# Block 0's low-rank adapters computed one batch at a time, in a fused adapter and feed-forward kernel

## The chip, the cores and the metric

The kernel runs on one core of one Trainium2 chip. The metric is the device time of one execution in microseconds (us), as the median of several runs. A profile is one execution recorded by the hardware; its span runs from the first to the last instruction of the program, and the execution's own time is a little longer than its span.

## What is computed

There are 8 batches of 256 tokens with 1024 features each. Every batch has an adapter number; two low-rank products (rank 16) with that adapter's matrices make the input of a gated feed-forward layer with 2752 hidden features, whose three inputs are rounded to 8-bit floating point. The result is added to `x`.

```python
def reference(x, adapter_ids, A, B, gate_w, up_w, down_w, scales...):
    Bx  = einsum('bni,bri->bnr', x, B[adapter_ids])      # 1024 -> 16
    c   = einsum('bnr,bor->bno', Bx, A[adapter_ids])     # 16 -> 1024
    q   = lambda v, s: clip(v / s, -448, 448).astype(float8_e4m3fn) * s
    gate_out = q(c, gate_in_scale) @ (gate_w * gate_w_scale).T
    up_out   = q(c, up_in_scale)   @ (up_w * up_w_scale).T
    hidden   = silu(gate_out) * up_out
    return x + q(hidden, down_in_scale) @ (down_w * down_w_scale).T
```

## The kernel before

All data is held transposed, features on the 128 partitions and tokens along the row. The 2048 tokens form four blocks `t` of 512 (`TB`), so a block holds two batches of 256 (`SEQ`). The 1024 features are eight groups `k` of 128 (`NH`); the 2752 hidden features are 22 chunks `c` (`NI`).

**Adapters of a block.** `times_b` (L483) multiplies x by the 16 rows of B. It puts four small products side by side on TensorE, each in its own quarter of 32 output rows; `quads` says which adapter, which tokens and which quarter. For block 0, `two_times_b` (L499) lets the quarters be (half of the batch) x (batch), 128 tokens each. The sums in PSUM (`bx`) are copied to `bm` in SBUF, once straight and once with the upper and lower quarters exchanged, since a quarter of `bm` must stand beside the quarter of `a_two` that it is multiplied with. `two_times_a` (L530) then makes the tiles `c`, eight of 512 columns for a block, and `round_to` (L523) rounds each to 8 bits in `xg[0]`, four on ScalarE (L528) and four on VectorE (L526).

**Loads.** `load_x` (L378) brings block 0's x in three pieces of 4, 3 and 1 groups `k` (`PIECES`, L39): 1 MB, 768 KB and 256 KB. `load_b` (L365) and `load_a_two` (L370) bring an adapter's B (68 KB) and A (two pieces of 32 KB, 16 rows each); their addresses hang on the adapter's number, which `adapter_of` (L362) reads into a register of the queue that will issue the transfer. `load_gate_up` (L385) brings a chunk of gate and up weights (`w_gu`, 1 MB; the first in two halves). All transfers are issued by SyncE (SP), in the order in which they are written, but for the numbers `ids` and the first B, which ScalarE issues:

```python
        load_x(0, 0)
        load_b(b_two[0], 0, adapter_of(0, nc.scalar), nc.scalar)
        second = adapter_of(1, nc.sync)
        load_b(b_two[0], 1, second, nc.sync)
        load_x(0, 4)
        load_a_two(0, 1, second)
        load_a_two(0, 0, adapter_of(0, nc.sync))
        load_x(0, 7)
        for c in range(NFIRST):
            load_gate_up(c, parts=1 if c else 2)
```

Every transfer signals one of eight completion semaphores, handed out in turn; a transfer that uses one again waits, on its issuing engine, until the transfer that had it before has landed. What stands behind it on that engine waits too.

**Order on TensorE.** Every matmul goes through `multiply` (L469), so all of them have line L470 in the profile, and TensorE keeps the written order (L633 to L653): 16 products of zeros 512 wide (`pass_time`, L472, tile `warm`), block 0's `two_times_b` with four more products of zeros after its fourth group, seven more, `two_times_a(0)`, then `gate_up(0, 0)`, which is chunk 0 for block 0, in four turns of two groups `k`; then chunks 1 to 4 for block 0, into the last of which block 1's `two_times_b` is put, block 1 likewise with the adapters of blocks 2 and 3, and then all other chunks for all blocks. Each `gate_up` is 16 matmuls of 512 columns.

**The down product.** For each group `k` of outputs, 21 matmuls and a rest per block go into `yd`; `finish` (L691) scales it, adds x on VectorE (L695) and issues the store of the tile. For the last group, x is loaded again by two transfers (L744 to L753) into the room of `xg`.

All tiles in PSUM come from one pool of eight buffers used in rotation.

Of the kernel before, what the change touches and what calls it, by code (L numbers as in the profile page):

```python
# [9 lines left out]
F32 = mybir.dt.float32  # L10
# [5 lines left out]
ALU = mybir.AluOpType  # L16
AX = mybir.AxisListType

P = 128
T = 2048  # L20
SEQ = 256
NB = 8
H = 1024
I = 2752
R = 16
NH = H // P
NI = (I + P - 1) // P
TAIL = I - (NI - 1) * P
TB = 512
# [6 lines left out]

KS = NH // 2

PIECES = ((4, 3, 1), (4, 3, 1), (NH,), (NH,))  # L39
FP8_MAX = 448.0  # L40

SAME_MAX = 240.0
# [14 lines left out]
    return ap.bitcast(U16)[..., 0::2]  # L57


def x_of(x4, t, k):  # L60

    first = 0
    for n in PIECES[t]:
        if k < first + n:
            break
        first += n
    at = (t * NH + first) * P * TB
    piece = x4[at : at + n * P * TB].rearrange("(p k n) -> p k n", p=P, k=n)
    return piece, first


def x_row(x4, t, k):
    piece, first = x_of(x4, t, k)
    return piece[:, k - first, :]


def gate_up_of(w_gu, c):
# [15 lines left out]
def general(  # L93
# [71 lines left out]
    def adapt(t, lora, b_sb, a_sb):  # L165
        bx = psum.tile([P, TB], F32, tag="ps", name="g_bx")
        for k in range(NH):
            xk = lora.tile([P, TB], F32, tag="xk", name="g_xk", bufs=2)
            nc.sync.dma_start(out=xk, in_=x_row(x4, t, k))
            nc.tensor.matmul(  # L170
                bx, lhsT=b_sb[:, k, :], rhs=xk, start=(k == 0), stop=(k == NH - 1)
            )
        bm = lora.tile([P, TB], F32, tag="bm", name="g_bm")
        for j in range(TB // SEQ):
            b = t * (TB // SEQ) + j
            nc.vector.tensor_scalar(
                bm[:, bass.ts(j, SEQ)],
                bx[:, bass.ts(j, SEQ)],
                mask[:, b : b + 1],
                None,  # L180
                ALU.mult,
            )
        for k in range(NH):
            c = psum.tile([P, TB], F32, tag="ps", name="g_c")
            nc.tensor.matmul(
                c, lhsT=a_sb[:, bass.ts(k, P)], rhs=bm, start=True, stop=True
            )
            for to, s in ((xg, GATE_IN), (xu, UP_IN)):
                v = work.tile([P, TB], F32, tag="v", name="g_v")
                nc.scalar.activation(v, c, AF.Copy, scale=inv[:, s : s + 1])  # L190
                quantize(to[:, k, :], v, P)
# [38 lines left out]
    def down(t, hid):  # L230
        for k in range(NH):
# [25 lines left out]
                    stop=(i == len(tail) - 1),  # L257
                )
            xr = work.tile([P, TB], F32, tag="g", name="g_xr")
            nc.sync.dma_start(out=xr, in_=x_row(x4, t, k))  # L260
            o = work.tile([P, TB], F32, tag="v", name="g_o")
            nc.vector.scalar_tensor_tensor(
                o, in0=y, scalar=down_s, in1=xr, op0=ALU.mult, op1=ALU.add
# [20 lines left out]
def adaln_ffn(  # L284
# [52 lines left out]
    with ExitStack() as fast:  # L337
# [2 lines left out]
        work = fast.enter_context(tc.tile_pool(name="work", bufs=3))  # L340


        xs = [acts.tile([P, NH, TB], F32, name=f"x{t}") for t in range(NTB)]
        xg += [acts.tile([P, NH, TB], FP8, name=f"xg{t}") for t in range(2, NTB)]


# [2 lines left out]

        b_two = [lora.tile([P, 2 * BROW + R], F32, name=f"b{t}") for t in range(2)]
        a_two = [lora.tile([P, H // 2], F32, name=f"a{t}") for t in range(2)]

        b_four = lora.tile([P, 4 * BROW + R], F32, name="b_four")
        a_four = lora.tile([P, H], F32, name="a_four")
        nc.gpsimd.memset(a_two[0], 0.0)
        nc.vector.memset(a_two[1], 0.0)
        for b, n in ((b_two[0], 2), (b_two[1], 2), (b_four, 4)):
            nc.vector.memset(b[:, n * BROW :], 0.0)  # L360

# [5 lines left out]
                out=b[:, i * BROW : (i + 1) * BROW], in_=b8[bass.ds(adapter * P, P), :]  # L367
            )

        def load_a_two(t, j, adapter):  # L370
            for g in range(2):
                row = 32 * (2 * g + j) + R * j
                nc.sync.dma_start(
                    out=a_two[t][row : row + R],
                    in_=a8[bass.ds(adapter * 2 * R + g * R, R), :],
                )

        def load_x(t, k):  # L378
            piece, first = x_of(x4, t, k)
            ks = slice(first, first + piece.shape[1])  # L380
            nc.sync.dma_start(out=xs[t][:, ks, :], in_=piece)

        w_of = {}

        def load_gate_up(c, parts=1):  # L385
# [5 lines left out]
                nc.sync.dma_start(out=w[:, bass.ts(i, n)], in_=src[:, bass.ts(i, n)])  # L391
            w_of[c] = w

        load_x(0, 0)
        load_b(b_two[0], 0, adapter_of(0, nc.scalar), nc.scalar)
        second = adapter_of(1, nc.sync)
        load_b(b_two[0], 1, second, nc.sync)


        load_x(0, 4)  # L400
        load_a_two(0, 1, second)
        load_a_two(0, 0, adapter_of(0, nc.sync))
        load_x(0, 7)
        for c in range(NFIRST):
            load_gate_up(c, parts=1 if c else 2)
        adapters = [adapter_of(2 + q, nc.sync) for q in range(6)]
        for j in range(2):
            load_b(b_two[1], j, adapters[j], nc.sync)
        for k in (0, 4, 7):
            load_x(1, k)  # L410
        for j in range(2):
            load_a_two(1, j, adapters.pop(0))

        for t in (2, 3):
            load_x(t, 0)
# [64 lines left out]
                    stop=(i == n - 1),  # L480
                )

        def times_b(bx, b, n, quads, between=None):  # L483


            for k in range(NH):
                for q, (i, row, t, cols) in enumerate(quads):
                    at = i * BROW + k * R - row
                    multiply(
                        bx[q][32 * q : 32 * (q + 1)],  # L490
                        lhsT=b[:, at : at + 32],
                        rhs=xs[t][:, k, cols],
                        start=(k == 0),
                        stop=(k == NH - 1),
                    )
                if between:
                    between(k)

        def two_times_b(t, between=None):  # L499


            n = SEQ // 2
            quads = [
                (j, R * j, t, slice(at, at + n))
                for half in range(2)
                for j in range(2)
                for at in (j * SEQ + half * n,)
            ]
            bx = [psum.tile([P, n], F32, tag="ps", name=f"bx{half}") for half in range(2)]
            times_b([bx[q // 2] for q in range(4)], b_two[t], n, quads, between)  # L510
            bm = lora.tile([P, 2, n], F32, tag="bm2", name="bm2", bufs=2)
            for other in range(2):
                for half, copy in enumerate((nc.vector.tensor_copy, nc.scalar.copy)):
                    to = half ^ other
                    tc.keep_in_program_order(
                        copy(  # L516
                            bm[64 * to : 64 * (to + 1), other],
                            bx[half][64 * half : 64 * (half + 1)],
                        )
                    )  # L520
            return bm

        def round_to(to, c, engine):  # L523
# [3 lines left out]
            else:  # L527
                nc.scalar.activation(to, c, AF.Copy, scale=scale, saturate=False)  # L528

        def two_times_a(t, bm):  # L530


            n = SEQ // 2
            for part in range(2):
                cs = [psum.tile([P, 2, SEQ], F32, tag="ps", name=f"c{q}") for q in range(4)]
                for other, i in product(range(2), range(2)):
                    for q in range(4):
                        rows = slice(32 * q, 32 * (q + 1))
                        multiply(
                            cs[q][:, i, bass.ts(q // 2 ^ other, n)],  # L540
                            lhsT=a_two[t][rows, bass.ts(2 * part + i, P)],
                            rhs=bm[rows, other],
                            start=True,
                            stop=True,
                        )
# [3 lines left out]
                    round_to(to, cs[q], nc.vector if q % 2 else nc.scalar)  # L549

        def four_times_b():
            quads = [(q, 0, 2 + q // 2, bass.ts(q % 2, SEQ)) for q in range(4)]
            bx = psum.tile([P, SEQ], F32, tag="ps", name="bx")
            times_b([bx] * 4, b_four, SEQ, quads)
            bm = lora.tile([P, SEQ], F32, tag="bm", name="bm", bufs=2)
            nc.vector.tensor_copy(bm, bx)
            return bm
# [73 lines left out]


        warm = psum.tile([P, TB], F32, tag="ps", name="warm")  # L633
        pass_time(warm, 16, TB)
        bm = two_times_b(0, lambda k: pass_time(warm, 4) if k == 3 else None)
        pass_time(warm, 7)
        two_times_a(0, bm)
        gate_up(0, 0, turns=(2, 2, 2, 2))
        for c in range(1, NFIRST - 1):
            gate_up(c, 0)  # L640
# [49 lines left out]

        def finish(k, t, cols, y, x):  # L691
            o = outs.tile([P, TB], F32, tag="o", name="o")[:, cols]
            at = slice(t * TB + cols.start, t * TB + cols.stop)
            tc.keep_in_program_order(
                nc.vector.scalar_tensor_tensor(  # L695
                    o, in0=y, scalar=down_s, in1=x, op0=ALU.mult, op1=ALU.add
                )
            )
            tc.keep_in_program_order(nc.sync.dma_start(out=outT[bass.ts(k, P), at], in_=o))
# [30 lines left out]
        for k in range(NH - 1):  # L730
# [9 lines left out]
            if last:  # L740
                ws_last = load_down(k + 1)
                x_last = []

                blocks = x4.rearrange("(t n) -> t n", t=NTB)  # L744
                srcs = (
                    blocks[:2, bass.ts(k + 1, P * TB)].rearrange("t (p n) -> p t n", p=P),
                    blocks[2:].rearrange("t (p k n) -> p t k n", p=P, n=TB)[:, :, k + 1, :],
                )
                for i in range(2):
                    x = xg[i].rearrange("p k n -> p (k n)").bitcast(F32)  # L750
                    x = x.rearrange("p (t n) -> p t n", n=TB)
                    x_last += [x[:, j, :] for j in range(2)]
                    nc.sync.dma_start(out=x, in_=srcs[i])  # L753
            first = k % 2 == 0
            if first:
                tiles = down_tiles(NTB)
# [128 lines left out]
```

## Time and profile before

| | |
|---|---|
| median of 3 runs | 476.82 us (476.09, 476.82, 476.93) |
| the profiled execution: its time, its span | 477.12 us, 475.3 us |
| TensorE busy with matmuls | 469.8 us (99% of the span), 2514 of them |
| ScalarE, VectorE busy | 192.5 us (40%), 105.6 us (22%) |
| first matmul of chunk 0 for block 0 starts | 12.58 us after the span's start |
| data moved | 53.44 MB, 112 GB/s over the span, about 400 GB/s from 3 us to 33 us |

Times within the profile are counted from the span's start. Busy shares are averages over the whole span; the change touches only the first 17 us, so it must be read in that stretch, from the order in time and from what each engine waits for.

### The profile page before, as it was taken

The page shows a single profiled execution, that of the slowest core. Times are in us where ns is not written, and L with a number is a line of the kernel's source. Part 1 is how long each engine was busy: PE and PEld are TensorE (multiplying, and loading weights), DVE is VectorE, ACT ScalarE, POOL GpSimd, SP SyncE. Part 2 cuts the span into 40 slices and gives each one's busy share as a digit, 9 for nine tenths or more (in the row PEclk, how much of TensorE's full clock was granted, in tenths as well). Part 3 has the DMA queues.
Part 4 walks back from the last instruction along what each step waited for, and adds up shares of the span by engine and source line. Part 5 has one row for each costly group of instructions (what it writes and reads, how often), then busy time and mean ns, then how long its engine had stood idle before and what let it go on. Part 6 is the DMA issues. An engine that isn't in the chain of part 4 may idle for free.

```text
span 475.3 us, 6009 instructions
## 1 busy us (share of the span) xinstructions
PE 469.8 (99%) x2514; PEld 217.0 (46%) x2514; DVE 105.6 (22%) x163; ACT 192.5 (40%) x249; POOL 1.0 (0%) x7
## 2 busy tenths in 40 slices
PE   8999999999999999999999999999999999999997
PEld 4454544444444444444444444444444444444444
DVE  1333432121212222121212212132120121031031
ACT  1322447995556654533454554359212022021000
POOL 0000000000000000000000000000000000000000
PEclk9999999999999999999999999999999999999999
DMA  8995013422222112222211111123335255063031
GB/s 291 406 405 186 1 48 133 176 88 90 88 88 89 24 66 89 90 88 88 90 30 60 44 62 56 61 83 123 103 146 161 64 185 161 22 213 114 3 116 66
DMA packets 13780, 53.44 MB, mean 112 GB/s; under 512 B 1650, under 2 KB 2930, under 8 KB 10674
## 3 DMA queue, kind: packets, MB, share of 16 engines
q1 hardware_dynamic: 13600, 52.92, 32.1%
q8 instruction: 21, 0.34, 0.3%
q14 instruction: 13, 0.11, 0.1%
q10 hardware_dynamic: 146, 0.07, 0.0%
HBM read 44.60 MB, written 8.39 MB: 111 GB/s over the span
## 4 chain that ended last, share of the span: by engine, by line
PE 96%; DMA 3%; SPq 0%; issue 0%; DVE 0%
PE y L470 62%; PE yd L470 31%; DMA w_gu<-w_gu 2%; PE c L470 1%; PE bx L470 1%; DMA x<-x 1%; DMA ids_i<-ids 0%; SPq L363 0%; SPq L366 0%; DVE o L695 0%; PE count L470 0%
## 5 line engine op out<-in xcount | busy, mean ns | idle before, releaser
L470 PE MATMUL y<-xg,w_gu 128*128 128x512 fp8e4 x1376 | 298.4, 379 | 0.9 <-DMA w_gu<-w_gu 0.9
L470 PEld LDWEIGHTS <-w_gu 128*128 128x128 bf16 x1376 | 134.0, 98 | 163.8 <-DMA w_gu<-w_gu 1.8
L470 PE MATMUL yd<-hid,w_d 128*128 128x512 fp8e4 (+2 forms) x693 | 146.0, 373 | 0.0
L609 ACT ACTIVATE g<-y,gate_s 128x512 f32<-128x512 f32 (+1 forms) x88 | 59.8, 681 | 137.2 <-PE y L470 137.2
L610 DVE SCALAR_TENSOR_TENSOR hid<-y,up_by_down,g 128x512 fp8e4<-128x512 f32 x84 | 63.1, 751 | 220.3 <-PE y L470 162.2
L470 PEld LDWEIGHTS <-w_d 128*128 128x128 bf16 x693 | 66.6, 98 | 79.0 <-issue 1.7
L456 ACT ACTIVATE junk<-w_d 128x1408 bf16<-128x1408 uint16 (+1 forms) x16 | 21.2, 1324 | 88.4 <-DMA w_d<-w_d 88.3
L695 DVE SCALAR_TENSOR_TENSOR o<-yd,down_s,x 128x512 f32<-128x512 f32 x28 | 20.0, 748 | 107.4 <-PE yd L470 92.8
L456 ACT ACTIVATE junk<-w_gu 128x2048 bf16<-128x2048 uint16 (+1 forms) x22 | 41.0, 1863 | 0.0
L463 ACT ACTIVATE junk<-hid 128x2048 bf16<-128x2048 fp8e4 x21 | 40.0, 1905 | 0.4
L463 ACT ACTIVATE junk<-xg 128x2048 bf16<-128x2048 fp8e4 x8 | 15.3, 1909 | 0.3
L528 ACT ACTIVATE xg<-c,inv 128x512 fp8e4<-128x512 f32 x16 | 9.7, 688 | 8.6 <-PE c L470 8.6
L526 DVE TENSOR_SCALAR xg<-c,inv 128x512 fp8e4<-128x512 f32 x16 | 10.9, 744 | 2.8 <-PE c L470 2.8
L470 PE MATMUL warm<-zeros 128*128 128x512 bf16 (+1 forms) x27 | 6.5, 402 | 1.2 <-DVE zeros L309 1.2
L695 DVE SCALAR_TENSOR_TENSOR o<-yd,down_s,xg 128x512 f32<-128x512 f32 (+2 forms) x5 | 3.2, 644 | 12.3 <-PE yd L470 12.3
L516 ACT COPY bm<-bx 64x128 f32<-64x128 f32 x4 | 1.0, 262 | 9.7 <-PE bx L470 9.6
L470 PE MATMUL bx<-x,b 128*32 128x128 f32 x128 | 4.3, 276 | 0.6 <-DMA x<-x 0.6
L470 PEld LDWEIGHTS <-zeros 128*128 128x128 bf16 x27 | 2.6, 116 | 4.7 <-issue 3.0
L470 PE MATMUL c<-bm,a 32*128 32x128 f32 x128 | 4.3, 277 | 0.0
L456 ACT ACTIVATION_READ_ACCUMULATOR junk<-w_gu 128x1 f32 x22 | 4.2, 191 | 0.0
L470 PEld LDWEIGHTS c<-bm,a 32*128 32x128 f32 x128 | 3.9, 186 | 0.5 <-ACT bm L516 0.4
L470 PE MATMUL yd<-hid_tail,w_dt 64*128 64x512 bf16 (+1 forms) x32 | 4.1, 377 | 0.0
(47 smaller groups left out, 41.0 us busy)
## 6 DMA issues: line engine op xcount, KB each, us to landing
w_gu<-w_gu SPq DMA_DIRECT2D x20, 1024.0 KB, 4.8
outT<-o SPq DMA_DIRECT2D x31, 256.0 KB, 2.2
w_d<-w_d SPq DMA_DIRECT2D x8, 704.0 KB, 4.8
w_d<-w_d SPq DMA_DIRECT2D x8, 640.0 KB, 3.9
x<-x SPq DMA_DIRECT2D x2, 2048.0 KB, 11.1
x<-x SPq DMA_DIRECT2D x2, 1024.0 KB, 8.6
x<-x SPq DMA_DIRECT2D x2, 768.0 KB, 9.5
w_gu<-w_gu SPq DMA_DIRECT2D x3, 512.0 KB, 3.8
```

What stands on the lines that cost most here:

```text
L456: nc.scalar.activation(junk_like(w), low(w), AF.Copy, accum_out=lows[:rows, column : column + 1])
L463: nc.scalar.activation(junk_like(q), q, AF.Square, accum_out=squares[:rows, column : column + 1])
L470: tc.keep_in_program_order(nc.tensor.matmul(*args, **kwargs))
L516: copy(bm[64 * to : 64 * (to + 1), other], bx[half][64 * half : 64 * (half + 1)],)
L526: nc.vector.tensor_scalar(to, c, scale, None, ALU.mult, saturate=False)
L528: nc.scalar.activation(to, c, AF.Copy, scale=scale, saturate=False)
L609: nc.scalar.activation(g[rows], gates, AF.Silu, scale=gate_s[: gates.shape[0]])
L610: nc.vector.scalar_tensor_tensor(to, in0=ups, scalar=up_by_down[rows], in1=g[rows], op0=ALU.mult, op1=ALU.mult, saturate=False,)
L695: nc.vector.scalar_tensor_tensor(o, in0=y, scalar=down_s, in1=x, op0=ALU.mult, op1=ALU.add)
```

## The change

Block 0's two batches are taken one after the other. The x of batch 0 lies ahead of that of batch 1 in memory and is loaded first, in two pieces of 512 KB; that of batch 1 follows in pieces of 896 KB and 128 KB. For each batch, `one_times_b` splits the 256 tokens in two halves and computes each half twice, in two quarters of the rows; all four quarters belong to one batch, so the copy to `bm` needs no exchange. The A of the batch is loaded into all four quarters of a tile of its own (four pieces of 32 KB instead of two). `one_times_a` makes tiles of 2 x 128 columns, so there are 16 roundings of 256 columns instead of 8 of 512. The B of both batches and half of the pieces of A are issued by ScalarE, the other half by SP. The zero products are 9 of 512 columns first, and three of 128 columns between B and A of each batch.

```diff
-PIECES = ((4, 3, 1), (4, 3, 1), (NH,), (NH,))
+PIECES = (      # first token, tokens, first k, ks
+    ((0, SEQ, 0, 4), (0, SEQ, 4, 4), (SEQ, SEQ, 0, 7), (SEQ, SEQ, 7, 1)),
+    ((0, TB, 0, 4), (0, TB, 4, 3), (0, TB, 7, 1)),
+    ((0, TB, 0, NH),), ((0, TB, 0, NH),),
+)
...
+        x_first = acts.tile([P, 2, NH, SEQ], F32, name="x0")
+        xs = [x_first.rearrange("p j k n -> p k j n")]
...
+        a_one = [lora.tile([P, H // 2], F32, name=f"a0{j}") for j in range(2)]
...
+        def load_a_half(a, q, g, j, adapter, queue):
+            row = 32 * q + R * j
+            queue.dma_start(
+                out=a[row : row + R], in_=a8[bass.ds(adapter * 2 * R + g * R, R), :]
+            )
...
         load_x(0, 0)
-        load_b(b_two[0], 0, adapter_of(0, nc.scalar), nc.scalar)
-        second = adapter_of(1, nc.sync)
-        load_b(b_two[0], 1, second, nc.sync)
-        load_x(0, 4)
-        load_a_two(0, 1, second)
-        load_a_two(0, 0, adapter_of(0, nc.sync))
-        load_x(0, 7)
+        load_x(0, 1)
+        queues = (nc.scalar, nc.sync)
+        numbers = [adapter_of(0, queue) for queue in queues]
+        load_b(b_two[0], 0, numbers[0], nc.scalar)
+        for q in range(4):
+            i = (q + 1) % 2
+            load_a_half(a_one[0], q, q % 2, 0, numbers[i], queues[i])
+        load_x(0, 2)
+        numbers = [adapter_of(1, queue) for queue in queues]
+        load_b(b_two[0], 1, numbers[0], nc.scalar)
+        for q in range(4):
+            i = (q + 1) % 2
+            load_a_half(a_one[1], q, q % 2, 1, numbers[i], queues[i])
+        load_x(0, 3)
         for c in range(NFIRST):
             load_gate_up(c, parts=1 if c else 2)
...
+        def one_times_b(j):
+            n = SEQ // 2
+            x = x_first[:, j]
+            quads = [(j, R * j, x[:, :, bass.ts(half, n)]) for half in (0, 0, 1, 1)]
+            bx = [psum.tile([P, n], F32, tag="ps", name=f"bx{half}") for half in range(2)]
+            times_b([bx[q // 2] for q in range(4)], b_two[0], n, quads)
+            bm = lora.tile([P, n], F32, tag="bm1", name="bm1", bufs=2)
+            for half, copy in enumerate((nc.vector.tensor_copy, nc.scalar.copy)):
+                rows = slice(64 * half, 64 * (half + 1))
+                tc.keep_in_program_order(copy(bm[rows], bx[half][rows]))
+            return bm
...
+        def one_times_a(j, bm):
+            n = SEQ // 2
+            for part in range(2):
+                cs = [psum.tile([P, 2, n], F32, tag="ps", name=f"c{q}") for q in range(4)]
+                for i, q in product(range(2), range(4)):
+                    rows = slice(32 * q, 32 * (q + 1))
+                    multiply(
+                        cs[q][:, i],
+                        lhsT=a_one[j][rows, bass.ts(2 * part + i, P)],
+                        rhs=bm[rows],
+                        start=True,
+                        stop=True,
+                    )
+                for g, half in product(range(2), range(2)):
+                    k = KS * part + 2 * g
+                    at = j * SEQ + half * n
+                    round_to(
+                        xg[0][:, k : k + 2, at : at + n],
+                        cs[2 * half + g],
+                        nc.vector if half else nc.scalar,
+                    )
...
-        pass_time(warm, 16, TB)
-        bm = two_times_b(0, lambda k: pass_time(warm, 4) if k == 3 else None)
-        pass_time(warm, 7)
-        two_times_a(0, bm)
+        pass_time(warm, 9, TB)
+        for j in range(2):
+            bm = one_times_b(j)
+            pass_time(psum.tile([P, TB], F32, tag="ps", name="warm"), 3)
+            one_times_a(j, bm)
         gate_up(0, 0, turns=(2, 2, 2, 2))
```

Three things follow elsewhere. `finish` reads block 0's x as two stretches of 256 columns. The x of the last group is loaded again by five transfers instead of two. And the turn of the completion semaphores moves: ahead of the first weights stand 15 transfers instead of 10. In the built program the second half of chunk 0 waits for the piece of 896 KB of x to land, and chunk 1 for the B of batch 1.

## The prediction

> **What bounds the kernel now.** I began with the chain that ended last, from the page's fourth part: it says whose time an edit must shorten.
>
> ```profile
> PE 96%; DMA 3%; SPq 0%; issue 0%; DVE 0%
> ```
>
> The end is set by TensorE, but for 3% of transfers, 14 us, all at the start. So I asked for the chain in order of time over the first 20 us (start, length, what).
>
> ```profile
> 3.33 4.97 DMA x<-x
> 8.30 0.02 issue
> 8.32 8.85 DMA w_gu<-w_gu
> 17.17 0.05 issue
> 17.21 2.98 PE y L470 x13
> ```
>
> Block 0's adapters are not in it. The chain runs through loads until 17.17, when chunk 1 of the weights lands; from then on TensorE works without a gap. The end is the landing of chunk 1 plus a rest of 458 us. The timeline of TensorE shows how much its own work is behind (start, length, idle before in brackets):
>
> ```profile
> 8.34 0.86 PE L470 MATMUL bx<-x,b 128*32 128x128 f32 x24 [0.22 <-DMA x<-x]
> 9.59 0.43 PE L470 MATMUL bx<-x,b 128*32 128x128 f32 x8 [0.38 <-DMA x<-x]
> 10.45 2.17 PE L470 MATMUL c<-bm,a 32*128 32x128 f32 x64
> 12.58 1.89 PE L470 MATMUL y<-xg,w_gu 128*128 128x512 fp8e4 x8
> 14.70 1.90 PE L470 MATMUL y<-xg,w_gu 128*128 128x512 fp8e4 x8 [0.23 <-DMA w_gu<-w_gu]
> 17.21 2.98 PE L470 MATMUL y<-xg,w_gu 128*128 128x512 fp8e4 x13 [0.62 <-DMA w_gu<-w_gu]
> ```
>
> After the adapters it waits twice more: 0.23 us for the second half of chunk 0 (14.65) and 0.62 us for chunk 1. Earlier adapters alone lengthen these waits; only earlier weights shorten the kernel. Last, the windows, for the transfers (last columns: clock, DMA share, GB/s):
>
> ```profile
> 6.00:7.00 1.00, 1.00 (x16) 0.46 (x18) 0.51 (x6) 0.00 (x0) 0.00 (x0) 1.00 0.98 412
> 7.00:8.00 1.00, 1.00 (x36) 0.75 (x24) 0.00 (x0) 0.00 (x0) 0.00 (x0) 1.00 0.92 275
> 8.00:9.00 1.00, 0.78 (x27) 0.59 (x24) 0.00 (x0) 0.00 (x0) 0.00 (x0) 1.00 0.85 293
> 9.00:10.00 1.00, 0.62 (x17) 0.21 (x10) 0.00 (x0) 0.00 (x0) 0.00 (x0) 1.00 0.99 387
> ```
>
> The queue is full but for a dip at 7 to 9 us: the third piece of x is issued at 6.62 only, its first bytes move at 8.25, and the engines ran dry at about 7.7 (the trace's record of packets). Issues and times to landing, by narrow windows: first x 0.75 + 5.0, B 2.88 + 3.2, second x 3.33 + 5.0, A 4.0 + 4.5, third x 6.62 + 2.9, chunk 0 7.09 + 3.8 and 7.56 + 7.1, chunk 1 8.32 + 8.9.
>
> One thing in it is odd. Chunk 0's second half took from 10.9 to 14.65, 3.7 us, for 512 KB that cost 1.3 us at 400 GB/s. Its 16 completions come at 11.7 to 12.3 for 13 of them, then at 13.1, 13.6 and 14.65; chunk 1's show the same tail (14.6 to 15.3, last 17.17). So three of the sixteen engines fell behind by up to 2.4 us at 11 to 14 us, and TensorE waits for the last one. I call this **the straggle**.
>
> **What the Trainium skill says.** "DMA: Bandwidth & Descriptors", section "Why a DMA increments its semaphore by 16 and not by 1": a transfer is spread over up to 16 engines and has landed only when all have counted. The straggle above agrees. The same page, section "Issuing engines are not separate DMA queues": a second issuing engine saves issue time only, since all transfers share the same 16 engines. The trace agrees: ScalarE's B, issued at 2.88, took 3.2 us behind the 1 MB of x, SP's at 2.92 took 3.3. "TensorE: Matmul & The Clock Gate", section "Part 1: The HAM clock gate": the array starts at half clock and gets the full one after about 3.4 us of sustained work, and falls back after an idle window of that length. The trace agrees on the first half: the zero products follow each other every 0.43 us up to about 5.2, four microseconds after the first, then in half of that. It shows no fall back.
>
> **The change, part by part.**
>
> *Bytes ahead of the weights.* Four more pieces of A, 4 x 32 KB. On each engine that is four packets of 2 KB at 84 ns (the trace's record of packets): **+0.34 us** for the weights. x in rows of 4 KB (159 ns) for 8 KB (309 ns) adds 16 x 159 - 8 x 309 = 72 ns. The last x piece, rows of 1 KB, is not shown; between 30 ns (its share of 4 KB) and 84 ns each, eight per engine; taken as 45.
>
> *Issue on SP.* Before the weights SP issues eight transfers and reads two numbers, both before and after, at about 0.4 us each; ScalarE issues five more, with nothing behind them on its queue until the copy to `bm` at 7 us. B of batch 0 and its first A go at 2.9 to 3.7, x of batch 1 at about 3.7. Then SP waits. Batch 1's A must wait for batch 0's A to land (about 6.3: behind the same 1 MB as B, 6.1 and 6.2 in the trace), so they go at 6.4 to 7.1, the last piece of x at 7.1 (6.62 before), the first half of chunk 0 at 7.5 (7.09). The dip stays: x of batch 1 ends at about 7.8, the last piece moves 1.3 to 1.6 us after its issue, 8.5. I take +0.15 us for chunk 0's start against before, bounds -0.5 (dip gone) to +0.5.
>
> *The new wait.* The second half of chunk 0 now waits for the 896 KB of x; behind it on SP stand chunks 1 to 4, and TensorE waits for all these. That piece runs from 5.3, at 8 x 271 ns per engine plus 0.3 of small pieces, to 7.8, and lands 0.5 us later, 8.3 to 8.8 (the second x landed at 8.33). Issue at 8.8 and 1.0 to 1.6 us to the first byte make 9.8 to 10.4. The engines have the last x and the first half of chunk 0 until about 10.3. So it is covered, just: 0 to 0.1 us; taken 0. Chunk 1's wait for B (issued by 5.4) is over before.
>
> The terms overlap, as the four extra pieces fill part of the dip. Two of the four (0.17), the longer rows (0.07) and half of the later issue are counted: **+0.25 us**, chunk 1 at 17.4.
>
> *TensorE.* Zero products end at 1.2 + 9 x 0.427 = 5.04 instead of 6.78. Batch 0's 32 products start with B, at 6.1, and end at 7.1; `bm`, eight tiles `c` and their roundings are done by 9.7, under the load of batch 1. Batch 1: x lands at 8.4 and 9.4, its last products end at 9.8, `bm` 0.35 later, first `c` at 10.4. A rounding of 256 columns lies between half and all of one of 512 (688 ns at L528, 741 at L526), taken as 0.45. `gate_up(0, 0)` needs one on each engine, and the first half of chunk 0 (10.9 + 0.25): first `y` at 11.3, against 12.58. Eight matmuls take 1.9 us as before. Then the second half is waited for, at 14.9: 1.7 us instead of 0.23. **The gain of 1.3 us on TensorE becomes waiting: 0.**
>
> *Elsewhere.* `finish` with two stretches: L695 takes 748 ns now; were it double, it would still lie under the 4.6 us that TensorE needs for a tile: 0. Three more loads of x for the last group: issued at 318, used at 460: 0. Block 1's x lands at 29.8 and 30.5 and its last products run at 31.2 and 31.9; both move with the queue: 0.
>
> Sum against the profiled execution: 477.12 + 0.25 = 477.37 us. It lies 0.30 above the median of the three runs, so the median becomes 476.82 + 0.25 = **477.1 us**.
>
> **The rivals.**
>
> *Faster: no straggle.* Nothing in the profile says that engines must fall behind. Before, TensorE would reach chunk 1 at 16.6 at the earliest, so a lucky execution gains 0.62 us at most; 477.12 - 0.62 - 0.23 = 476.3, near the fastest run, 476.09. After, it would be ready at 11.3 + 3.8 = 15.1, and chunk 1 lands at 14.9 + 0.25. All of 17.2 - 15.3 = 1.9 us can then come out: 474.9; with half of the straggle 475.9. For it: one run in three looks like that, and issues and packets move. Against: two of three runs and the profiled one don't. Middle 475.3.
>
> *Slower: the wait for the 896 KB.* SP issues no weights until all sixteen parts of that piece are there. The point is its landing at about 9.0: later than that, the engines run dry after the first half of chunk 0, microsecond for microsecond. If one falls behind by 1.2 us there (half of the straggle) and the straggle comes too, chunk 1 lands at 18.4 to 18.6: 478.2. For it: the trace shows engines 2.4 us behind, and the wait is new. Against: the pieces of x before 9.6 show at most 0.6 us between first and last part.
>
> *Slower: the clock.* Nine zero products end 0.2 us before the clock rose; if it rises only in a later window, the products and chunk 0 run at half speed, TensorE is ready for chunk 1 at up to 18.3 instead of 17.4: 478.0.
>
> *The change doesn't do what it says:* the built order shows both batches' products apart, so no.
>
> **How the numbers follow.** Small shift 0.50 (its own range 476.2 to 477.7), no straggle 0.20, wait for x 0.22, clock 0.08. A measurement of this kernel can tell about 0.2% (0.95 us) from no change, so faster 0.2, same 0.5, slower 0.3. The range takes in most of both sides, to 475.3 and 478.6; what lies outside is a full gain of 1.9 us and both delays at once.
>
> **What would show it.** Right: first `y` near 11.3, a wait for the second half of chunk 0 of 1 us or more, chunk 1 within 0.7 us of 17.4, no gap later. Wrong: `y` running through to chunk 1 by 15.5; a hole in the DMA row at 10 us; zero or B products at twice their spacing after 6 us; or TensorE waiting for block 1's x at 30 us.

## The result, and the profile after

The change made the kernel slower: a median of 481.21 us (479.94 to 481.49) against 476.80 us, a ratio of 1.0085 with a 95% interval of 1.0068 to 1.0101. The forecast was 477.1 us, within 475.3 to 478.6. The profiled execution took 481.49 us, its span is 479.7 us (475.3 before).

I read the profile in the same order as before. First the chain that ended last, from the page:

```profile
PE 97%; DMA 1%; ACTq 1%; ACT 0%; issue 0%; DVE 0%
```

The share of transfers has fallen from 3% to 1%, although the kernel is slower. In order of time (start, length, what), the chain of the first 60 us has

```profile
5.17 5.38 DMA b<-b
...
10.60 0.43 PE bx L491 x8
11.02 0.27 PE warm L491 x3
11.29 0.15 issue
11.44 2.21 PE c L491 x31
13.65 2.54 PE bx L491 x64
...
18.15 16.56 PE y L491 x76
34.71 1.89 PE bx L491 x64
```

The loads of x and of weights are gone from it. What is left is one transfer of a B, which ScalarE issued at 5.17 behind its other issues, and then block 0's adapters, which were not in the chain before. From 18.15 on TensorE has no gap. A good mark for all that follows is the start of block 1's B products, the last row: 34.71, against 30.34 in the chain before. The difference, 4.37 us, is that of the spans (4.4), and from this mark to the end all kernels here need the same 445 us, within about 0.4. So the loss lies ahead of it, in TensorE's timeline (start, length, idle before in brackets):

```profile
6.75 1.74 PE L491 MATMUL bx<-x,b 128*32 128x128 f32 x56 [1.74 <-DMA b<-b]
10.60 0.43 PE L491 MATMUL bx<-x,b 128*32 128x128 f32 x8 [2.11 <-DMA b<-b]
...
11.44 2.21 PE L491 MATMUL c<-bm,a 32*128 32x128 f32 x32
13.58 2.59 PE L491 MATMUL bx<-x,b 128*32 128x128 f32 x64
...
16.55 1.48 PE L491 MATMUL c<-bm,a 32*128 32x128 f32 x32
18.15 14.19 PE L491 MATMUL y<-xg,w_gu 128*128 128x512 fp8e4 x65
```

Three things are to be seen. First, batch 0's B products stop after seven of eight groups `k` (56 records of 64) and wait 2.11 us for a B, though batch 0's own B had released them at 6.75. It is batch 1's B, issued at 5.17 and landed at 10.55. `times_b` reads B in windows of 32 columns that start at `i * BROW + k * R - row`; for batch 0 and `k` = 7 these are columns 112 to 143, and with `BROW` = 136 the last eight belong to batch 1. They only fill rows that meet zeros in A, but TensorE waits for them. Before, both B's had landed by 6.25 us, and nothing showed. Second, a batch has 64 records of B products; before, both batches together had 64: 24 and 8 in lines that the prediction shows, and ahead of them

```profile
6.71 1.08 PE L470 MATMUL bx<-x,b 128*32 128x128 f32 x32
```

Third, the first A products take 2.21 us and the second 1.48, for the same 32 records. The windows tell why (after the window's length TensorE's busy time, ..., then granted clock, DMA share and GB/s at the end):

```profile
9.00:10.00 1.00, 0.00 (x0) 0.00 (x0) 0.00 (x0) 0.00 (x0) 0.00 (x0) 1.00 0.09 24
10.00:11.00 1.00, 0.41 (x9) 0.21 (x10) 0.00 (x0) 0.00 (x0) 0.00 (x0) 1.00 0.62 170
11.00:12.00 1.00, 0.85 (x16) 0.71 (x16) 0.28 (x1) 0.26 (x1) 0.00 (x0) 0.76 0.96 291
12.00:13.00 1.00, 1.00 (x26) 1.00 (x25) 0.21 (x1) 0.41 (x2) 0.00 (x0) 0.50 0.77 266
```

TensorE is idle at 9 to 10 us, and the clock falls to one half, by the trace's record of the clock from 11.5 to 14.9. The same rows show the hole in the transfers: 24 GB/s at 9 to 10 us. SP's own waits explain it (total, times, longest):

```profile
SPq L384 <- DMA a<-a: 2.0, 1, 2.0
SPq L394 <- DMA a<-a: 1.4, 1, 1.4
...
SPq L404 <- DMA x<-x: 0.2, 1, 0.2
```

SP stood still until pieces of batch 0's A had landed, the last of them at 9.32; the wait for the 896 KB of x (last row) was 0.2 us. The last piece of x was issued at 9.34 and the first half of chunk 0 at 9.74; chunk 1 was issued at 10.74 and landed 8.6 us later, at 19.35 instead of 17.17. But TensorE came to it only at about 21.6 (18.15 and 16 matmuls of 0.216), so this delay did not show in the end.

### The profile page after: what moved, and what is told of

Its sections match the earlier page's. It is cut to its first block, busy times and chain, and to the rows that moved or that the text cites. A ratio compares the mean times of both kernels' runs of the same rounds, so it can differ in the third digit from the quotient of the medians.

```text
span 479.7 us, 6152 instructions
## 1 busy us (share of the span) xinstructions
PE 471.4 (98%) x2566; PEld 219.7 (46%) x2566; DVE 106.8 (22%) x168; ACT 193.2 (40%) x253; POOL 1.0 (0%) x7
## 4 chain that ended last, share of the span: by engine, by line
PE 97%; DMA 1%; ACTq 1%; ACT 0%; issue 0%; DVE 0%
PE y L491 62%; PE yd L491 31%; PE c L491 2%; PE bx L491 2%; DMA b<-b 1%; ACT L313 0%; ACTq L384 0%; ACTq L375 0%; ACTq L378 0%; ACTq L312 0%; DVE o L753 0%; DVE bm L528 0%; PE warm L491 0%; PE count L491 0%
## 5 line engine op out<-in xcount | busy, mean ns | idle before, releaser
L560 ACT ACTIVATE xg<-c,inv 128x512 fp8e4<-128x512 f32 (+1 forms) x20 | 10.5, 601 | 9.8 <-PE c L491 9.7
L558 DVE TENSOR_SCALAR xg<-c,inv 128x512 fp8e4<-128x512 f32 (+1 forms) x20 | 11.6, 638 | 4.2 <-PE c L491 4.2
L491 PE MATMUL bx<-x,b 128*32 128x128 f32 x192 | 6.7, 293 | 3.8 <-DMA b<-b 3.8
L491 PEld LDWEIGHTS bx<-x,b 128*32 128x32 f32 x192 | 5.6, 119 | 5.5 <-issue 2.4
L491 PE MATMUL c<-bm,a 32*128 32x128 f32 x128 | 5.8, 318 | 0.3
L491 PE MATMUL warm<-zeros 128*128 128x512 bf16 (+1 forms) x15 | 4.5, 455 | 1.2 <-DVE zeros L315 1.2
L491 PEld LDWEIGHTS c<-bm,a 32*128 32x128 f32 x128 | 5.2, 219 | 1.0 <-ACT bm L548 0.4
```

The costliest lines, as they stand in the source:

```text
L491: tc.keep_in_program_order(nc.tensor.matmul(*args, **kwargs))
L558: nc.vector.tensor_scalar(to, c, scale, None, ALU.mult, saturate=False)
```

## The experiments

Four causes were to be told apart: the wait for batch 1's B, the clock, the arithmetic batch by batch, and the loads with their waits. Ratios are to the kernel before, with 95% intervals; the median of before beside them was 476.7 to 476.8 us.

**e1: the B's set apart**

```diff
-BROW = NH * R + 8
+BROW = NH * R + 16
...
-    rest = np.broadcast_to(np.pad(scales, (0, 2)), (8 * P, 8))
+    rest = np.broadcast_to(np.pad(scales, (0, 10)), (8 * P, 16))
```

> The changed kernel with one edit: the two B's of block 0 stand 144 columns apart instead of 136, so that batch 0's last 32-column window of B (columns 112 to 143) no longer touches the columns of batch 1's B. Theory 1 (TensorE's wait of 2.1 us at batch 0's last group k is for batch 1's B, which batch 0 does not need; with it goes the idle time that let the clock fall): batch 0 is done by 10.5 us, the clock stays at 1.00, first y near 14, and the end is then set by the landing of chunk 1, which stays at about 19.3 because SP still waits as before: 476.8 + 2.1 = 478.9 us. Rival, the clock alone (it falls because only 9 zero products stand at the start): the clock still falls near 11 us and the time stays above 480.5. Rival, the doubled products of B are the cost: the time stays above 480.

Measured: 479.02 us, ratio 1.0037 (1.0027 to 1.0047). The interval is clear of that of the changed kernel: this one false wait, with the fall of the clock behind it, cost about half of the loss, 0.48% or 2.3 us. TensorE's timeline of e1:

```profile
6.91 3.44 PE L491 MATMUL bx<-x,b 128*32 128x128 f32 x64 [1.69 <-DMA b<-b]
10.28 0.34 PE L491 MATMUL warm<-zeros 128*128 128x128 bf16 x3
10.76 1.29 PE L491 MATMUL c<-bm,a 32*128 32x128 f32 x32
12.01 2.31 PE L491 MATMUL bx<-x,b 128*32 128x128 f32 x64
...
16.11 14.19 PE L491 MATMUL y<-xg,w_gu 128*128 128x512 fp8e4 x65
```

The time is what I had expected, but not for my reason. The first `y` came at 16.1, not 14, and ran past chunk 1's landing (18.4) without a wait: TensorE set the end, not the weights. Batch 0's B products took 3.44 us. The views of tile `bx` give minimum, median and maximum of one record in ns; the first is e1 from 6.8 to 10.2 us, the second the kernel before from 6.5 to 8. The medians are 421 and 273:

```profile
L491 PE MATMUL bx<-x,b x64: 273/421/421, 6.9 to 10.1; 128*32 128x128 f32 x64
...
L470 PE MATMUL bx<-x,b x32: 272/273/297, 6.7 to 7.5; 128*32 128x128 f32 x32
```

In this execution the clock had not risen when the nine zero products were over, and rose at 10.0 (the trace's record).

**e2: TensorE kept busy in the waits**

```diff
+            fill = (lambda k: pass_time(warm, 40) if k == NH - 1 and not j else None)
...
-        pass_time(warm, 9, TB)
+        pass_time(warm, 13, TB)
```

> The changed kernel with every wait left as it is, but TensorE kept busy in them: 13 instead of 9 zero products of 512 columns at the start, and 40 of 128 columns ahead of batch 0's last group k. Theory 1 (the wait for B and the clock are two costs): clock 1.00, batch 0's last group still at about 10.6 us, but its A products, batch 1's B and A products run at full speed: first y near 16.3 instead of 18.15, 481.2 - 1.7 = 479.5 us. If the clock were the whole cost: below 478. If the clock were no cost: 481.

Measured: 480.05 us, ratio 1.0059 (1.0041 to 1.0077); the interval just overlaps that of the changed kernel. In the trace the clock stays at 1.00:

```profile
10.20 0.42 PE L491 MATMUL bx<-x,b 128*32 128x128 f32 x8
...
16.53 16.56 PE L491 MATMUL y<-xg,w_gu 128*128 128x512 fp8e4 x76
```

Batch 1's B had landed at 9.72 here; the zero products held the last group until 10.20. From the last group to the first `y` it takes 6.33 us instead of 7.55. The changed kernel's own executions say the same: three of the four, with a mean granted clock of 0.996, took 481.07 to 481.49 us, and the fourth, with 1.000, took 479.94, which is e2's time. So somewhat over 1 us of the 2.3 is the half-speed stretch behind the wait, and the rest, about 1 us by subtraction, the wait itself.

**e7: e1 with 16 zero products**

```diff
-        pass_time(warm, 9, TB)
+        pass_time(warm, 16, TB)
```

> As e1 (B's 144 columns apart), with 16 zero products of 512 columns at the start instead of 9. In e1's trace batch 0's products of B ran at half speed until 10.0 us, since the clock had not risen by the end of the nine zero products. Theory (clock, products done twice and late weights are three separate costs): the clock is up before batch 0, its B products take 1.95 us instead of 3.44, first y near 14.5 instead of 16.1; then TensorE waits for the second half of chunk 0 and for chunk 1, which lands at 18.4 to 19.3: 476.8 + 1.3 to 2.1 = 478.0 to 478.9 us, at least 0.3 below e1. Rival (the clock does not matter once batch 1's B is no longer waited for): first y at 16, 479.0 as e1.

Measured: 479.20 us, ratio 1.0047 (1.0029 to 1.0065), not below e1: the expected 0.3 us did not come. The profiled execution (478.94 us) ran as expected up to the first `y`; its timeline of TensorE:

```profile
6.66 1.96 PE L491 MATMUL bx<-x,b 128*32 128x128 f32 x64
...
10.73 1.95 PE L491 MATMUL bx<-x,b 128*32 128x128 f32 x64 [0.41 <-DMA b<-b]
...
14.72 3.61 PE L491 MATMUL y<-xg,w_gu 128*128 128x512 fp8e4 x16
18.65 11.62 PE L491 MATMUL y<-xg,w_gu 128*128 128x512 fp8e4 x52 [0.32 <-DMA w_gu<-w_gu]
```

With the clock up (by the products' durations; this trace has no record of the clock), batch 0's B products take 1.96 us and the first `y` comes at 14.72, 1.4 us before e1's. Then the late weights show: chunk 1 is waited for until 18.6, chunk 2 until 22.3, and block 1's B products start at 32.00, only 0.67 ahead of e1. Batch 1's products, too, could not begin before 10.6: the 0.41 us in their row is a wait for their own B, which landed at 10.60. These limits lie close together, so taking one away gives little. In single executions of e1 (477.93 to 479.62) and e7 (477.98 to 479.49) the spread is larger than that difference; the two can't be ranked.

**e11: the arithmetic alone** (`one_times_b` and `one_times_a` as in the changed kernel, B's set apart as in e1; of each A only two of the four quarters are loaded)

```diff
...
-        bm = two_times_b(0, lambda k: pass_time(warm, 4) if k == 3 else None)
-        pass_time(warm, 7)
-        two_times_a(0, bm)
+        for j in range(2):
+            bm = one_times_b(j)
+            pass_time(psum.tile([P, TB], F32, tag="ps", name="warm"), 3)
+            one_times_a(j, bm)
```

> The loads of the kernel before, in its order and on its queues (B's 144 columns apart), with the changed kernel's arithmetic batch by batch and 16 zero products at the start. Only two of the four quarters of each A are loaded, the other two stay zero, so block 0's result is wrong in half of its tokens. Theory (the B products, done twice, and the two chains one after the other are a cost of their own on TensorE: 3.9 us of B products for 1.95): batch 0's chain ends at about 11.5, batch 1's B products run 11.5 to 13.4, first y near 15.3 against 12.58, chunk 1 started at about 19 without a wait for w_gu: 478.3 to 478.8 us. Rival (only the loads and their waits cost time, the arithmetic hides under them): 476.7 to 477.2.

Measured: 479.53 us, ratio 1.0056 (1.0041 to 1.0072), slower by 0.7 us than the upper end that I had given. TensorE's timeline of e11:

```profile
10.15 0.43 PE L480 MATMUL bx<-x,b 128*32 128x128 f32 x8 [0.36 <-DMA x<-x]
10.51 0.34 PE L480 MATMUL warm<-zeros 128*128 128x128 bf16 x3
10.99 1.17 PE L480 MATMUL c<-bm,a 32*128 32x128 f32 x32
12.23 2.31 PE L480 MATMUL bx<-x,b 128*32 128x128 f32 x64
14.47 0.34 PE L480 MATMUL warm<-zeros 128*128 128x128 bf16 x3
14.74 1.32 PE L480 MATMUL c<-bm,a 32*128 32x128 f32 x32
16.27 13.97 PE L480 MATMUL y<-xg,w_gu 128*128 128x512 fp8e4 x64 [0.21 <-DVE xg L548]
```

From the last x products of batch 0 to the first `y` it takes 6.1 us, where the kernel before needed 3.0 (9.59 to 12.58). Batch 1's B products, 2.31, are most of the 3.1 us more; its chain of zero products, copy and A is the rest. Nothing waits for weights; chunk 1 landed at 16.5. Two limits of this run: the last x landed at 10.11, 0.56 later than in the profile before, so some of the 2.75 us need not be arithmetic; and in this order of loads both batches wait for the same last piece of x, so nothing of the arithmetic could hide. That it hides under these loads is out; how much hides in the changed kernel's order, e11 can't say.

**e8: the loads alone** (the pieces of A go to the quarters where the arithmetic of the kernel before looks for them)

```diff
...
-        pass_time(warm, 9, TB)
-        for j in range(2):
-            bm = one_times_b(j)
-            pass_time(psum.tile([P, TB], F32, tag="ps", name="warm"), 3)
-            one_times_a(j, bm)
+        pass_time(warm, 33, TB)
+        bm = two_times_b(0)
+        pass_time(psum.tile([P, TB], F32, tag="ps", name="warm"), 7)
+        two_times_a(0, bm)
```

> The changed kernel's loads, in its order and with its queues and waits, but the arithmetic of the kernel before (both batches together, B products once, eight roundings of 512 columns), and 33 zero products of 512 columns ahead, so that the clock stays up while x is awaited. Theory (SP's new waits alone cost about 2 us, through chunk 1's landing): B products from 10.4 us on, first y near 14.3, chunk 1 lands at about 19: 478.6 to 479.0 us, with TensorE waiting for w_gu. Rival (the loads cost nothing by themselves; the changed kernel is slow through its arithmetic on TensorE): below 477.3.

Measured: 478.96 us, ratio 1.0045 (1.0030 to 1.0060). The size is as expected, the way only partly. TensorE's timeline of e8:

```profile
1.19 10.10 PE L491 MATMUL warm<-zeros 128*128 128x512 bf16 x33 [1.19 <-DVE zeros L315]
11.23 1.95 PE L491 MATMUL bx<-x,b 128*32 128x128 f32 x64
...
15.74 14.63 PE L491 MATMUL y<-xg,w_gu 128*128 128x512 fp8e4 x67
```

Chunk 1 landed at 18.2, 1.0 us late, but TensorE came to it at 19.3, since the last piece of x had landed at 11.0 only, 1.5 us later than before, and the zero products ran until 11.2. So in e8 the loads cost through x, and the filler has a share: the 896 KB of x had landed by 9.67, when the second half of chunk 0 was issued. By an estimate from these times and 1.74 us for seven groups (changed kernel), the B products could have ended at 11.8 instead of 13.2. TensorE would then have waited for chunk 1, and about 1.0 us would be left of the 2.2. The loads alone cost between the two.

**e5: the weights issued sooner** (e1, with batch 1's A left to ScalarE)

```diff
...
-            i = (q + 1) % 2
-            load_a_half(a_one[1], q, q % 2, 1, numbers[i], queues[i])
         load_x(0, 3)
-        for c in range(NFIRST):
-            load_gate_up(c, parts=1 if c else 2)
+        for c in range(2):
+            load_gate_up(c, parts=1 if c else 2)
+        for q in range(4):
+            load_a_half(a_one[1], q, q % 2, 1, numbers[0], nc.scalar)
+        for c in range(2, NFIRST):
+            load_gate_up(c)
```

> The B's 144 columns apart as in e1, and batch 1's A all issued by ScalarE, so that SP issues the last piece of x and chunk 0 without waiting for batch 0's A to land in between. Theory (SP's waits for landed pieces delay the weights, and so set the end once TensorE no longer waits for B): the last x and the first half of chunk 0 go at about 7 us instead of 9.34 and 9.74, chunk 1 lands 1 to 2 us earlier than 19.3, TensorE is ready for it at about 17.5 to 18: 477.2 to 478.2 us. Rival (the weights' landing is set by bytes and stragglers alone, not by their issue): chunk 1 at 19.3 again, 478.9 as e1.

Measured: 478.38 us, ratio 1.0034 (1.0023 to 1.0045), not to be told from e1. The last x went at 6.00 and the first half of chunk 0 at 6.43, as meant; but the second half still waited for the 896 KB, until 10.06, and chunk 1 for batch 1's B, until 11.84, and it landed at 18.2, hardly earlier. Block 1's B products started at 32.44, and TensorE waited for no weights (first `y` 15.87; the clock rose at 9.8, as late as in e1). It leaves open what the waits on SP would cost if all were gone.

**e9: the kernel before with nine zero products**

```diff
-        pass_time(warm, 16, TB)
+        pass_time(warm, 9, TB)
```

> The kernel before with 9 instead of 16 zero products of 512 columns at the start. Theory (nine end before the clock has risen for sure, and the wait for B that follows keeps it down): in some or all executions block 0's B and A products run at half speed; they are 2 us each at full speed, so first y comes 1 to 3 us later than 12.58, and as only 0.85 us of waiting follow, the time rises by 0.5 to 2 us: 477.3 to 478.8. Rival (the clock rises anyway by about 5.2 us): 476.8.

Measured: 477.20 us, ratio 1.0010 (1.0000 to 1.0020), 476.02 to 479.43 in single executions. The profiled one (476.47) had the full clock in time. Six of its 20 executions lie above 477.75 us, where all but one of 33 of the kernel before stay at or below it. That suggests that nine are a gamble, of which the median shows little; no slow execution was profiled, so that the clock is the cause of all six isn't shown.

**e6, e10 and e12: the kernel before with x in other pieces.** They follow the dip at 7 to 9 us and chunk 1's landing.

```diff
-PIECES = ((4, 3, 1), (4, 3, 1), (NH,), (NH,))
+PIECES = ((4, 4), (4, 3, 1), (NH,), (NH,))      # e6, e10; e12: (6, 2)
...
-        load_x(0, 7)
...
# e6 only: x first, all small loads by ScalarE
+        load_x(0, 4)
+        numbers = [adapter_of(j, nc.scalar) for j in range(2)]
+        for j in range(2):
+            load_b(b_two[0], j, numbers[j], nc.scalar)
+        for j in range(2):
+            load_a_two(0, j, numbers[j], nc.scalar)
```

> The kernel before with block 0's x in two pieces of 1 MB, both issued first, and all small loads of block 0 issued by ScalarE; the x of the last group is loaded again by four transfers. Theory (before, the end is chunk 1's landing, and the queue ran dry at 7.7 to 8.2 us since the third x was issued at 6.62): no dip, chunk 0 issued at about 6 us, chunk 1 lands near 16.3 and TensorE is ready for it at about 16: 475.9 us. Rival (stragglers set the landing, whatever the issue): 476.8.

> The kernel before with block 0's x in two pieces of 1 MB instead of 1 MB, 768 KB and 256 KB, all else as it was (the x of the last group is loaded again by four transfers). Theory (before, the end is set by chunk 1's landing, and the queue runs dry at 7.7 us as the third piece is issued at 6.62): the dip goes, chunk 0 is issued at 6.6, chunk 1 lands about 0.5 us earlier, TensorE is ready at 16.5: 476.3 us. Rival (TensorE's products of the last four groups come later and take the gain back, or stragglers set the landing): 476.8 or more.

> The kernel before with block 0's x in two pieces of 6 and 2 groups (1.5 MB, 512 KB), 18 zero products, the four zero products after the sixth group, and the x of the last group loaded by four transfers. In e10 nothing waited for weights any more, and TensorE's own chain set the end: its products of the last four groups took 1.08 us after x landed at 9.2. Theory: only two groups are left after the second piece lands, 0.5 us less; first y near 12.35, no wait for weights: 476.1 us, 0.5 below e10. Rival (first piece lands too late, or stragglers in chunk 1 come back): 476.6 or more.

Measured: e6 480.38 us, ratio 1.0067 (1.0038 to 1.0096); e10 476.57 us, 0.9991 (0.9979 to 1.0003); e12 476.92 us, 1.0004 (0.9996 to 1.0013). e6 failed by a thing that the prediction itself had cited: its B's, issued at 3.5 and 4.0 by the other queue, landed only at 10.0 and 10.2, behind 2 MB of x and the first half of chunk 0 (512 KB), all of which SP had issued by 1.93. The wait of e6's TensorE:

```profile
PE bx L467 <- DMA b<-b: 2.6, 1, 2.6
```

Behind this wait, too, the clock fell to one half, from 10.25 to 13.66 by the trace's record; the first 32 records of B products took 2.02 us instead of 1.08.

In e10 chunk 1 landed at 14.6 and TensorE never waited for weights; the bound moved to TensorE's own chain (first `y` at 12.85, later than before's 12.58), and the gain of 0.16 us is within the interval. e12 did not shorten it (12.81). So no version here is shown to beat the kernel before.

## Why the prediction was wrong

*What bounds the kernel before* stands, as a bound that lies close to the next one. With chunk 1 at 14.6, e10 was rid of both waits (0.23 and 0.62 us), yet gained next to nothing, since TensorE's own chain (first `y` at 12.85) lies right behind.

*The part "TensorE" failed, twice.* First, "Batch 0's 32 products start with B, at 6.1, and end at 7.1": I took 1.0 us for 32 instructions, reading the 32 records of 1.08 us as such. `times_b` issues 8 groups times 4 quarters, 32 instructions, and the trace has 64 records of them, so one leaves two; the 32 instructions of a block before are the 64 records, 1.95 us where they follow each other (block 1). The change issues 32 for each batch, and each batch takes 1.96 (e7). The term was 2.0 us for both batches and is 3.9. From B at 6.1 to the first `y` at 11.3 I had 5.2 us; in e7, with the clock up and no wait but one of 0.41 us, TensorE needed 8.1 (6.66 to 14.72). e11 priced the whole arithmetic, with nothing to hide under: 2.75 us.

Second, the same sentence assumed that batch 0 needs its own B only. In the part "Issue on SP" this stands as "with nothing behind them on its queue until the copy to `bm`": nothing stood behind batch 1's B on ScalarE, but TensorE did. Together with the clock it cost 2.3 us (e1), somewhat over 1 of it the clock (e2).

"The gain of 1.3 us on TensorE becomes waiting: 0" is therefore wrong in sign: first `y` came 5.57 us later. From there to the mark of block 1's B products it took 16.56 us instead of 17.76, since the two waits and breaks of the kernel before were gone; 5.57 - 1.20 is the 4.37 us of the spans.

*The part on loads* had the mechanism and missed the size. SP's waits were named; A was to land at 6.3, and the pieces issued by ScalarE took longer, one until 9.32. So +0.25 us for chunk 1 became 2.2 (17.17 to 19.35). Block 0's own loads were late as well: the 896 KB landed at 10.35 (predicted: 8.3 to 8.8), batch 1's B at 10.55, the last x at 11.55 (predicted: 9.4). So batch 1's products could not have ended at 9.8 even with the count right and without the false wait.

*The rivals.* The 896 KB did land past the point of about 9.0 that was given, at 10.35, with its last part 0.9 us behind the one before (9.46), and chunk 1 landed later than the 18.4 to 18.6 given. But that wait held SP for 0.2 us only: the hole at 9 to 10 us is SP's wait for a piece of A, which stands ahead of it. Neither set the end. The clock's rival named the right resource: the clock fell after an idle stretch in the changed kernel and rose late in e1, for up to 1.5 us on batch 0's B products. The Trainium skill ("TensorE: Matmul & The Clock Gate", "Part 1: The HAM clock gate") says that it falls back after an idle window of about 3.4 us; the trace of before didn't show a fall, the windows of the changed kernel do, though its idle stretch was 2.1 us only. The mistake was to price each rival alone: late loads, the clock and a cause not listed came in one execution.

*How the parts add up.* Arithmetic alone cost 2.75 us (e11) and loads alone 2.2 (e8), each with the reservations made there, and both together 2.3 to 2.5 (e1, e7). They need not add: e7's timeline has batch 0's chain from 6.66 to 10.32, before batch 1's B landed, as the change meant. The rest of the 4.4, about 2 us, is the false wait and the clock. What stays open: why one ScalarE piece of A needs until 9.3, what the loads would cost without SP's waits, and what an earlier issue of batch 1's B would give, which no run tried.

## What to carry to other kernels

Before a chain is split so that its first half can start early, follow every operand of the first half to the columns it truly reads: a padded or overlapping window ties it to the second half's load, which costs nothing only as long as both loads come together. Count instructions in the built program, and durations over the same instructions in the profile, before taking a price for "the same work": what fills idle quarters of an array by doing work twice is not free where that array is about to become the bound. And where a first stage waits, ask what the idle time does to the clock of the stage behind it.

## What the runs showed of the hardware

By the traces' records of the clock, its rise isn't fixed by the number of zero products: with nine it came at 4.7 us in the changed kernel, 5.3 in e9, 10.0 in e1, and with sixteen at 5.2 in the kernel before and 6.0 in e11. In the changed kernel it fell at 11.5 after a stretch of 8.5 to 10.6 without a matmul, and stayed down for 3.4 us; in e6 it fell at 10.25 after one of 7.6 to 10.2, for 3.4 us as well. The kernel before isn't safe from it: of its 96 executions beside the experiments three had a mean granted clock of 0.996, and they took 479.8 to 480.0 us, 3 us over its median. In no run here did a B issued by ScalarE land before what SP had already queued: 68 KB of it needed 3.2 us behind 1 MB of x (kernel before) and 6.6 us behind 2.5 MB of x and weights (e6).
